# Sixteen-field blocks of a pairwise product: one level of steps replaced by four-by-four products, 18 VectorE instructions a tile instead of 22

## The chip, the cores and the metric

One core of a Trainium2 chip. The experiments ran in three batches on three chips (e1 to e4, e5 to e8, e9 to e11), each with runs of the kernel before on the same chip. The metric is device time in microseconds of one execution. Most executions of a kernel agree within 0.3%.

## The reference

```python
# x: (4096, 32, 64) float32, W: (64, 64) float32
vid = jnp.einsum('bfd,de->bfe', x, W)
idx_i, idx_j = jnp.triu_indices(32, k=1)          # 496 pairs i < j
return x[:, idx_i, :] * vid[:, idx_j, :]          # (4096, 496, 64): 520 MB
```

Some 34 MB go in and 520 MB come out, with one multiplication for each number that is written, besides the product with W, which TensorE does.

## The kernel before

The batch is cut into 16 tiles. In a tile 128 partitions hold the 64 embedding dimensions of two halves of the batch, and the free dimension is fields by C = 128 batch rows. TensorE puts vid for all 32 fields into PSUM. VectorE multiplies x and vid into an output buffer of SLOT = 124 pairs; there are three such buffers, used in turn, and a tile of 496 pairs fills four of them one after the other. SyncE's queue sends each full buffer out (8.13 MB). The order in which pairs are computed is free, since the host puts them in place, so the kernel picks orders that let one instruction do many pairs. A "row" is a rectangle of pairs: each of several fields with the same run of other fields. A "step" is one column of pairs in each of several equal groups of fields.

```python
def by_field():                       # the first two tiles
    return [("row", j, 0, 1, j) for j in range(1, 32)]

def by_block():                       # the other fourteen
    def within(lo):                   # the pairs inside sixteen fields
        yield "step", lo, 2, 1, 0
        for k in range(2):
            yield "step", lo, 4, 2, k
        for k in range(4):
            yield "step", lo, 8, 4, k     # 2 groups x 4 pairs in one instruction
        yield "row", lo + 8, lo, 8, 8     # 8 x 8 pairs in one instruction
    yield from within(0)
    yield "row", 16, 0, 16, 16
    yield from within(16)
...
    opool = ctx.enter_context(tc.tile_pool(name="out", bufs=3))
...
        if 0 < t < NT - 1:
            loaded.append(load(t + 1, 4, nc.scalar))   # four loads of 512 KB
...
            nc.vector.tensor_tensor(o, left, right, ALU.mult)      # line 159
            at += n
            if t * NP + at == until or at in (base + SLOT, NP):
                nc.sync.dma_start(out=out[t][:, sent:at, :],
                                  in_=ot[:, sent - base : at - base, :])
```

A row is split where a buffer ends, which is why a tile had 22 products. The first two tiles send smaller pieces, so that transfers start early.

## Time and profile before

| | before |
|---|---|
| time, median of 3 (range) | 1296.04 us (1294.44 to 1296.83) |
| VectorE busy | 1087.2 us of 1295.9, 376 instructions |
| VectorE idle ahead of line 159, waiting | 124.3 us output landings, 37.3 us "issue", 7.5 us TensorE |
| bytes moved | 553.80 MB, 427 GB/s over the span |
| landing of a full buffer (its transfer is complete) | 43.4 us after its issue |

The second and the fourth row pull in opposite directions: is it the engine that is busy for 84% or the traffic? An average over the span can't say.

### The profile page before, as it was taken

The numbers are of one execution on the slowest core, as the hardware profiler recorded it, in microseconds if no ns is written. First come the engines' busy times: TensorE is split into PE (matmuls) and PEld (weight loads), VectorE is DVE, ScalarE is ACT, GpSimd is POOL, SyncE is SP. The second block draws the span as 40 slices with busy tenths as digits, with TensorE's granted clock in tenths as the row PEclk, the third lists the DMA queues.
The fourth block names the chain that finished last, engine by engine and source line by source line (L and its number), as shares of the span: only waits on it lengthen the run. The fifth ranks groups of instructions, "written<-read, shape, count | busy, mean of one in ns | idle before, by whom it ended". The sixth has DMA issues, their size and how long they took to land.

```text
span 1295.9 us, 1845 instructions
## 1 busy us (share of the span) xinstructions
PE 229.7 (18%) x512; PEld 48.5 (4%) x512; DVE 1087.2 (84%) x376; POOL 0.2 (0%) x4
## 2 busy tenths in 40 slices
PE   4112022112122121221212212122121221212000
PEld 1000000000000000000000000000000000000000
DVE  7999999788798887978879888798897978978870
POOL 0000000000000000000000000000000000000000
PEclk8555555555555555555655555555555555655555
DMA  9999999999999999999999999999999999999996
GB/s 390 431 422 439 427 431 450 432 423 439 430 434 429 425 438 434 424 432 429 435 432 432 433 433 433 434 432 433 435 432 432 431 432 432 430 431 445 437 425 276
DMA packets 20890, 553.80 MB, mean 427 GB/s; under 512 B 2448, under 2 KB 2448, under 8 KB 10256
## 3 DMA queue, kind: packets, MB, share of 16 engines
q1 hardware_dynamic: 12816, 524.33, 93.8%
q10 hardware_dynamic: 8064, 29.36, 5.5%
q8 instruction: 4, 0.07, 0.0%
q14 instruction: 6, 0.05, 0.0%
HBM read 33.59 MB, written 520.09 MB: 427 GB/s over the span
## 4 chain that ended last, share of the span: by engine, by line
DMA 55%; DVE 39%; issue 2%; PE 0%; DVEq 0%; SPq 0%
DMA out_dram<-o 55%; DVE o L159 39%; DMA x<-in_r_x_dram 0%; PE vid L134 0%; DVEq L200 0%; DVEq L159 0%; SPq L111 0%
## 5 line engine op out<-in xcount | busy, mean ns | idle before, releaser
L159 DVE TENSOR_TENSOR o<-x,vid 128x1024 f32<-128x1024 f32 (+15 forms) x376 | 1087.2, 2963 | 169.1 <-DMA out_dram<-o 124.3
L134 PE MATMUL vid<-x,w 64*64 64x512 f32 x512 | 229.7, 1032 | 958.6 <-DMA x<-in_r_x_dram 601.8
L134 PEld LDWEIGHTS vid<-x,w 64*64 64x64 f32 x512 | 48.5, 205 | 1138.1 <-DVE o L159 637.3
L182 POOL MEMSET const-uint8-127<- 128x1 uint8 x1 | 0.1, 103 | 0.0
L182 POOL MEMSET const-bfloat16-1.0<- 128x1 bf16 x1 | 0.1, 102 | 0.0
L182 POOL MEMSET const-float32-1.0<- 128x1 f32 x1 | 0.1, 100 | 0.0
L182 POOL MEMSET const-float32-0.0<- 128x1 f32 x1 | 0.1, 99 | 0.2 <-issue 0.2
## 6 DMA issues: line engine op xcount, KB each, us to landing
out_dram<-o SPq DMA_DIRECT2D x56, 7936.0 KB, 43.4
x<-in_r_x_dram ACTq DMA_DIRECT2D x56, 512.0 KB, 45.5
out_dram<-o SPq DMA_DIRECT2D x2, 3008.0 KB, 18.2
out_dram<-o SPq DMA_DIRECT2D x1, 5952.0 KB, 27.5
out_dram<-o SPq DMA_DIRECT2D x1, 4928.0 KB, 23.6
out_dram<-o SPq DMA_DIRECT2D x1, 4416.0 KB, 19.5
out_dram<-o SPq DMA_DIRECT2D x1, 4224.0 KB, 21.6
out_dram<-o SPq DMA_DIRECT2D x1, 3904.0 KB, 15.8
```

What stands on the lines that cost most here:

```text
L134: nc.tensor.matmul(vid[half, b : b + BANK, :], lhsT=w2[half, :], rhs=xt[half, b : b + BANK, :], start=True, stop=True,)
L159: nc.vector.tensor_tensor(o, left, right, ALU.mult)
L182: nc = _bacc.Bacc("TRN2", target_bir_lowering=False, num_devices=1, dynamic_dma_scratch_size=1024)
```

## The change

The intent is to do the same multiplications in fewer, larger VectorE instructions. Within eight fields, the pairs of the upper four with the lower four are a 4 x 4 block. Before, four "step" instructions did one column of that block each, for both groups of eight fields at once. Now each block is one "row" instruction.

```diff
-        for k in range(4):
-            yield "step", lo, 8, 4, k
+        for i in (lo, lo + 8):
+            yield "row", i + 4, i, 4, 4
```

## The prediction

> **What bounds the kernel now.** I read the page first: busy shares, then the 40 slices, then the chain of waits. After it come the groups of instructions kept apart by shape, the chain in order of time, and ten-microsecond windows over the handover to the blocked tiles and over the end. These are the page's lines:
>
> ```profile
> PE 229.7 (18%) x512; PEld 48.5 (4%) x512; DVE 1087.2 (84%) x376; POOL 0.2 (0%) x4
> ...
> DVE  7999999788798887978879888798897978978870
> ...
> DMA  9999999999999999999999999999999999999996
> GB/s 390 431 422 439 427 431 450 432 423 439 430 434 429 425 438 434 424 432 429 435 432 432 433 433 433 434 432 433 435 432 432 431 432 432 430 431 445 437 425 276
> DMA packets 20890, 553.80 MB, mean 427 GB/s; under 512 B 2448, under 2 KB 2448, under 8 KB 10256
> ...
> DMA out_dram<-o 55%; DVE o L159 39%; DMA x<-in_r_x_dram 0%; PE vid L134 0%; DVEq L200 0%; DVEq L159 0%; SPq L111 0%
> ```
>
> VectorE's 84% tempts one to cut its work. But its row in the slices has gaps from the eighth slice to the end, while the DMA row is 9 in every slice but the last, and moves 422 to 450 GB/s in all but the first and the last. Two engines can't both be the bound; the one without gaps is. The chain says 39% VectorE and 55% output transfer, which needs its order in time (start, length, what):
>
> ```profile
> 899.56 16.76 DVE o L159 x2
> ...
> 1017.58 43.47 DMA out_dram<-o
> 1061.08 0.05 DVEq L159
> 1061.17 16.76 DVE o L159 x2
> 1077.95 43.69 DMA out_dram<-o
> ```
>
> A transfer of 43 us frees a buffer, VectorE fills it in 17 us, its transfer takes 43 us again. A buffer holds 124 products: 124 x 128 x 128 x 4 bytes = 8.13 MB, and at 432 GB/s that is 18.8 us. A landing of 43 us is therefore a queue: the transfer stands behind two others of the three buffers. So the chain's VectorE share is largely not time that VectorE costs: while it fills one buffer, the transfers of the other two are under way or queued.
>
> The period confirms it. The piece at 1061.17 has its like at 899.56, eight buffers or two tiles earlier: (1061.17 - 899.56) / 2 = 80.8 us a tile. A tile moves 496 x 65,536 bytes = 32.51 MB out and 32 x 65,536 = 2.10 MB in, 34.60 MB; over 80.8 us that is 428 GB/s. VectorE has less to do in it. These rows give shape, count, busy us with mean ns, and idle us before it:
>
> ```profile
> L159 DVE TENSOR_TENSOR o<-x,vid 128x14336 f32<-128x14336 f32 x28 | 422.3, 15084 | 44.5 <-DMA out_dram<-o 44.5
> L159 DVE TENSOR_TENSOR o<-x,vid 128x8192 f32<-128x8192 f32 x28 | 243.1, 8681 | 0.0
> L159 DVE TENSOR_TENSOR o<-x,vid 128x1024 f32<-128x1024 f32 x198 | 226.6, 1215 | 38.4 <-issue 37.3 <-DMA out_dram<-o 1.1
> L159 DVE TENSOR_TENSOR o<-x,vid 128x1536 f32<-128x1536 f32 x32 | 56.0, 1750 | 36.7 <-DMA out_dram<-o 36.7
> L159 DVE TENSOR_TENSOR o<-x,vid 128x512 f32<-128x512 f32 x32 | 21.9, 684 | 42.2 <-DMA out_dram<-o 42.0 <-PE vid L134 0.2
> L159 DVE TENSOR_TENSOR o<-x,vid 128x2176 f32<-128x2176 f32 x4 | 9.7, 2415 | 0.0
> L159 DVE TENSOR_TENSOR o<-x,vid 128x1920 f32<-128x1920 f32 x2 | 4.3, 2147 | 0.0
> ```
>
> A blocked tile is 2 x 15.084 + 2 x 8.681 + 14 x 1.215 + 2 x 1.750 + 2 x 0.684 = 69.4 us by these means (67.9 us from first start to last end in the timeline, since neighbours overlap a little). So VectorE idles some 11 to 13 us of each 80.8 us. All of that idle sits ahead of shapes that open a new buffer (14336, 1024, 1536, 512), and none ahead of the 8192 shape, which never does. The part named "issue", 37.3 us in 12 pieces, lies at the first product of a tile, which waits for a buffer, TensorE and VectorE together; with 3.1 us a piece it is as long as the other buffer waits (124.3 us in 40 pieces), and I read it as the same wait.
>
> **What the Trainium skill says.** "Perfetto Trace Analysis", section "Roofline", gives about 435 GB/s as the ceiling of one core's 16 DMA engines when the core beside it is idle. The trace agrees: 429 to 435 GB/s in most slices, and 432 over the 960 us from 220 to 1180. "DMA: Bandwidth & Descriptors", section "Issuing engines are not separate DMA queues", says that transfers issued by different engines interleave on the same 16. The trace fits: loads from ScalarE's queue take 45.5 us for 512 KB, as long as outputs fifteen times larger, and total GB/s stays at the same level. "VectorE: DVE Perf Modes", section "The TRN2 errata", puts an fp32 tensor_tensor of N elements at (N+151)/0.96 ns: 1224 ns for 1024 against 1215 here, so the fixed part of 151/0.96 = 157 ns is nearly confirmed although one operand here is in PSUM.
>
> **The change, part by part.** It touches only the part inside blocks of sixteen fields. Four products of 2 x 4 pairs (1024 elements a partition) become two of 4 x 4 pairs (2048 elements), twice a tile. On TensorE, on ScalarE's and on SyncE's queue the order of instructions and their waits are the same in both programs; on VectorE eight 1024 instructions a tile become four of 2048. The first two tiles, which go field by field, don't change. The bytes, transfers, buffers and cut points of the output don't either: each buffer still ends at 124 products.
>
> Fixed cost of an instruction, from the trace: (15084 - 8681) / 6144 = 1.042 ns an element, and 1215 - 1024 x 1.042 = 148 ns. The new shape is then 2048 x 1.042 + 148 = 2282 ns; the mean of the 1920 and 2176 rows, (2147 + 2415) / 2 = 2281 ns, says the same. Two old ones cost 2430 ns, so each pair saves 148 ns. Fourteen tiles x 4 = 56 instructions fewer: 56 x 0.148 = 8.3 us of VectorE, 0.59 us a tile. Access patterns with one more level cost nothing extra in the trace: 8192 and 14336, which have both operands broadcast over a level, lie on the line of the plain shapes.
>
> Where these 0.59 us lie: 0.3 us in the first buffer of a tile and 0.3 us in the last. Both are between two waits for a landing. From about 212 us to the end VectorE is already ahead, so the wait gets longer by what the work gets shorter: on the path, 0. Before that, from about 130 us, VectorE runs without a gap for one blocked tile. These windows give length, busy times by engine, clock, DMA share, GB/s:
>
> ```profile
> 150.00:160.00 10.00, 0.00 (x0) 0.00 (x0) 10.00 (x3) 0.00 (x0) 0.50 1.00 430
> 160.00:170.00 10.00, 3.68 (x8) 0.84 (x8) 10.00 (x4) 0.00 (x0) 0.50 0.99 420
> 170.00:180.00 10.00, 3.68 (x8) 0.84 (x8) 10.00 (x2) 0.00 (x0) 0.67 1.09 471
> ```
>
> VectorE is full, but so are the transfers, so the 0.59 us of this tile only makes the queue longer: 0 again. At the end, VectorE starts the last buffer at 1239.1 us and finishes at 1256.3. At 1239.1, by the chain in order of time, the transfer of the tile's first buffer has landed and two remain: 2 x 18.8 us, so the last one could start at about 1276.7, 20 us after it was issued, and end at about 1295.5, which is the span. Being issued 0.3 us earlier doesn't end it earlier. Sum on the path: 0 to -0.6 us.
>
> **The rivals.** First, VectorE bounds after all, as 84% busy and 39% of the chain suggest, and the whole 8.3 us shows: 1287.7 us, 0.64% less. Against it: 161.6 us of waits for buffers, in 52 of the 56 buffers of the blocked tiles. Even so it would be within 2%. Second, the 4 x 4 form runs slower than the line, through broadcasts on both operands: at twice the rate cost, 56 x 2.13 = 119 us more VectorE work, 8.5 us a tile, still under the idle of 11 to 13 us, so about 1298 us. The 8 x 8 shape, built by the same branch of the code, speaks against it. Third, the shift in reads frees PSUM and x earlier or later and loads collide differently with outputs. VectorE waited on TensorE only twice, 7.5 us in total, at the start, and fields 4 to 7 and 20 to 23 are released sooner, so TensorE can only gain slack; bytes are the same, and I give this 1 us either way. Fourth, the slowest of the DMA engines decides the end: the last windows fall from 444 to 165 GB/s at 1280 us, with single packets to the end, so engines don't finish together. That tail may vary by some microseconds from run to run, and is the largest part of my range.
>
> ```profile
> 1270.00:1280.00 10.00, 0.00 (x0) 0.00 (x0) 0.00 (x0) 0.00 (x0) 0.50 1.02 444
> 1280.00:1290.00 10.00, 0.00 (x0) 0.00 (x0) 0.00 (x0) 0.00 (x0) 0.50 0.38 165
> ```
>
> **Range and chances.** The centre is 1296.0 less half of 0.6, rounded: 1295.7 us. The three runs before spread over 2.4 us, another chip or day may add as much, and the first rival would take up to 8 us off: 1292 to 1299 us. Over 2% faster would need 26 us, three times all that the change removes from VectorE, so 0.005; over 2% slower needs the new form to cost well beyond the second rival, about 0.01. Within 2%: 0.985.
>
> **What would show it.** VectorE x320 and not x376; busy 1087.2 - 8.3 = 1078.9 us, a share of 83%; 56 of the new 2048 shape near 2282 ns and 86 of 1024; VectorE's idle up from 169.1 to about 177 us, nearly all on output landings; the tile period still 80.8 us; the DMA row still 9; output landings still near 43 us, and the wait ahead of the last buffer longer by about 0.3 us. I am wrong if the period falls by about 0.6 us a tile (first rival), if the 2048 rows are near 4000 ns (second), or if GB/s in the middle slices moves from about 432 (third).

## The result, and the profile after

The changed kernel took 1294.8 us (median of 4, 1292.93 to 1296.52) beside 1295.24 us (1293.92 to 1296.83) of the kernel before. The ratio is 0.9996, with an interval of 0.9977 to 1.0015: the same.

The page of the changed kernel, with the parts that answer to those shown before: busy time, slices, traffic, chain.

```profile
PE 227.8 (18%) x512; PEld 48.5 (4%) x512; DVE 1083.6 (84%) x320; POOL 0.2 (0%) x4
...
DVE  7999999888898887888879788798887988979870
...
DMA  9999999999999999999999999999999999999996
GB/s 393 429 423 438 429 432 435 430 431 434 433 434 431 432 433 435 433 435 436 433 431 436 431 433 431 435 434 431 431 431 434 431 433 427 427 431 438 438 430 302
...
DMA out_dram<-o 55%; DVE o L159 39%; DMA x<-in_r_x_dram 0%; PE vid L134 0%; DVEq L200 0%; DVEq L159 0%; SPq L111 0%
```

The 56 instructions are gone, and nothing else looks different: the same gaps in VectorE's row, a full DMA row, the same rate, the same shares of the chain. But busy time fell by 3.6 us only (1087.2 to 1083.6), not by 8.3. The groups kept apart by shape (count, then busy us with mean ns, then idle ahead) show that the new shape cost what was expected of it:

```profile
L159 DVE TENSOR_TENSOR o<-x,vid 128x2048 f32<-128x2048 f32 x56 | 125.4, 2280 | 0.0
L159 DVE TENSOR_TENSOR o<-x,vid 128x1024 f32<-128x1024 f32 x86 | 99.8, 1215 | 40.3 <-issue 38.1 <-DMA out_dram<-o 2.2
```

The mean of 2280 ns is within 2 ns of the prediction. Busy time is not count times mean here, though: 56 x 2.280 = 127.7, and the row says 125.4; for 1024 elements 86 x 1.215 = 104.5, and the row says 99.8. The first number counts the time that instructions cover together, and neighbours overlap. The timeline of VectorE shows it for the last buffer of the run, start and length first, then the count and the wait ahead. This is the kernel before:

```profile
1239.11 17.20 DVE L159 TENSOR_TENSOR o<-x,vid 128x512 f32<-128x512 f32 x9 [1.92 <-DMA out_dram<-o]
```

And this the changed one:

```profile
1236.53 17.07 DVE L159 TENSOR_TENSOR o<-x,vid 128x512 f32<-128x512 f32 x7 [1.93 <-DMA out_dram<-o]
```

Two instructions fewer shorten the same 124 products by 0.13 us, 65 ns each. The earlier start can't be put down to the change from one pair of profiles: it is the 2.5 us by which the two profiled executions differ as a whole, and executions of the kernel before alone lay between 1292.54 and 1296.64 us in one batch. The chain in order of time has its old rhythm:

```profile
897.72 16.76 DVE o L159 x2
...
1015.74 43.26 DMA out_dram<-o
...
1059.12 16.76 DVE o L159 x2
1075.90 43.57 DMA out_dram<-o
```

Two tiles take 1059.12 - 897.72 = 161.40 us, 80.7 us a tile, where the kernel before took 80.8. A saving on the path of 0.26 us a tile (3.6 us over 14) is the size of the differences between neighbouring periods, so this view alone can't exclude it. The experiments have to.

### The profile page after: what moved, and what is told of

The parts are those of the page before. It is cut to its first block, busy times and chain, and to the rows that moved or that the text cites. A ratio compares the mean times of both kernels' runs of the same rounds, so it can differ in the third digit from the quotient of the medians.

```text
span 1293.4 us, 1789 instructions
## 1 busy us (share of the span) xinstructions
PE 227.8 (18%) x512; PEld 48.5 (4%) x512; DVE 1083.6 (84%) x320; POOL 0.2 (0%) x4
## 4 chain that ended last, share of the span: by engine, by line
DMA 55%; DVE 39%; issue 2%; PE 0%; DVEq 0%; SPq 0%
DMA out_dram<-o 55%; DVE o L159 39%; DMA x<-in_r_x_dram 0%; PE vid L134 0%; DVEq L200 0%; DVEq L159 0%; SPq L111 0%
## 5 line engine op out<-in xcount | busy, mean ns | idle before, releaser
L159 DVE TENSOR_TENSOR o<-x,vid 128x2048 f32<-128x2048 f32 (+13 forms) x320 | 1083.6, 3454 | 170.0 <-DMA out_dram<-o 124.2
```

## The experiments

Labels e1 to e11 are the order of the runs; here they are grouped by question. Theory: the 16 DMA engines bound the kernel from some 5 us after the start to the end; VectorE has about 3 us to spare in each of the 56 buffers, so neither adding nor removing less than that changes the time. Rival 1: VectorE bounds, wholly or in part, and the saving was just too small to see. A second question is why the saving was 3.6 us and not 8.3: the theory formed from the trace is that the mean duration of an instruction holds some 83 ns that lie over its neighbour, so that an instruction removed gives back only about 65 ns.

### More and less work for VectorE

Extra products go to a spare tile, K of them in each buffer of the fourteen blocked tiles. VectorE's own order was fixed to that of the program, which leaves the changed kernel's instructions as they were.

```diff
             nc.vector.tensor_tensor(o, left, right, ALU.mult)
+            if t >= 2 and at == base:
+                for _ in range(K):
+                    nc.vector.tensor_tensor(extra, xt[:, 0:8, :], xt[:, 8:16, :], ALU.mult)
```

K = 2 (e1):

> The changed kernel with two extra VectorE products of 1024 elements in each of the 56 buffers of the blocked tiles, written to a spare tile. The result stays correct. Each extra product waits for the one before, so a pair costs about 2.4 us a buffer, 56 x 2.4 = 134 us of VectorE. Theory (the 16 DMA engines bound, VectorE idles 2.9 us a buffer): all of it goes into the idle, which falls from 170 to about 35 us; time 1295 us, within 4 us of the kernel before. Rival (VectorE bounds): 1294.8 + 134, about 1429 us.

Measured: 1297.21 us (1294.62 to 1297.47), ratio to the kernel before 1.0011 (0.9995 to 1.0028), so the same. VectorE's busy time rose from 1083.6 to 1214.7 us. Here are the page's busy line and VectorE's waits for this run (line 159 has become 160; us in total, times, longest):

```profile
PE 224.7 (17%) x512; PEld 51.4 (4%) x512; DVE 1214.7 (94%) x432; POOL 0.2 (0%) x4
```

```profile
DVE o L160 <- DMA out_dram<-o: 26.9, 28, 2.8
DVE o L160 <- PE vid L135: 8.4, 2, 7.8
DVE o L160 <- issue: 6.9, 10, 0.8
```

The waits of the changed kernel were 124.2, 7.7 and 38.1. So 131 us of added work came out of 128 us of waiting, and the time hardly moved. It also fits the reading of "issue" as a wait for buffers: it shrank together with the named one, from 3.2 us a piece to 0.7.

K = 5 (e2):

> As the run with two extra products, but five in each buffer: about 6.1 us a buffer, 343 us of VectorE, more than the idle of 162 us that lies ahead of buffers. Theory: VectorE becomes the bound, its waits for landings go to about 0 and the time is 1295 + (343 - 162) + some us, 1450 to 1490 us. Rival (VectorE bounded all along): 1295 + 343, about 1638 us.

Measured: 1455.48 us, ratio 1.1238. VectorE's work rose by 333 us against the changed kernel; the time by 161 us. Now the two rows of the slices change roles:

```profile
DVE  7999999999999999999999999999999999999994
...
DMA  9999998979889888898987988979899797897878
```

The gaps are in the DMA row, and this trace has no wait for an output landing at all. With some 7.6 us of short gaps, the last product ended at 1432.4 us and not at 1253.6, 178.8 us later: the work added (333.4) less the waits that it filled (162.2), and the gaps. About 19 us came back at the end, where fewer transfers were still queued after that product (21 us from there to the end of the span, and 39.8 in the changed kernel). Together the two runs place the threshold between 131 and 333 us of added work, with the position that the idle time gives, 162 us, explaining the second to within its tail.

The other direction takes work away from VectorE, far more than the change did: the two large products of each tile become ScalarE copies (e4).

```diff
-            nc.vector.tensor_tensor(o, left, right, ALU.mult)
+            if t >= 2 and m == 7:
+                nc.scalar.copy(o, left)          # wrong result on purpose
+            else:
+                nc.vector.tensor_tensor(o, left, right, ALU.mult)
```

> The changed kernel with the two 14336-element products of each blocked tile taken from VectorE; ScalarE, which was idle, copies x into their place (wrong result on purpose). VectorE loses 28 x 15.08 = 422 us, a third of the span; bytes and buffers stay. Theory: the time stays within 5 us of 1295 us and VectorE's idle grows by about 420 us. Rival (VectorE's share of the chain is real cost): a fall by up to 39% of the span, at least by 100 us.

Measured: 1296.2 us (1292.47 to 1296.85), ratio 0.9998 (0.9976 to 1.0021). VectorE was busy for 663.9 us, 51% of the span, and waited 583.2 us for output landings:

```profile
PE 228.8 (18%) x512; PEld 48.4 (4%) x512; DVE 663.9 (51%) x292; ACT 341.2 (26%) x29; POOL 0.2 (0%) x4
```

```profile
DVE o L162 <- DMA out_dram<-o: 583.2, 54, 18.6
```

A hundred times the saving of the change also bought nothing, within the 3 us that the interval leaves open. That is the strongest reading of what VectorE's work costs. It has a limit: a copy took ScalarE 12.1 us, so in 28 of the 56 buffers the filling became shorter by 4.6 us only (16.75 to 12.1) and did not vanish.

### The change undone and more (e5)

```diff
-        for ... in products(by_field() if t < 2 else by_block()):
+        for ... in products(by_field()):
```

> The change undone and more: all sixteen tiles go field by field, 34 products a tile and not 18, with the same bytes and buffers. 14 x 16 = 224 instructions more. At the marginal 65 ns that the two traces give (3.6 us of busy time for 56 instructions) it is 14.6 us of VectorE, at the 148 ns of the prediction 33 us; the idle of 162 us takes either. Theory: same as before, 1294 to 1297 us, VectorE busy about 1098 us (at 148 ns: 1117 us). Rival (VectorE bounds): 1309 to 1328 us.

Measured: 1297.33 us (1294.84 to 1299.1) beside 1296.1, ratio 1.0016 (0.9999 to 1.0033): the same, and a tenth of a per cent can't be excluded: the median is 0.3 us above the range expected. This is not the kernel before: the whole blocked order is gone, and not the change alone. VectorE's busy time was 1097.9 us, 14.3 us over the changed kernel: 14.3 / 224 = 64 ns an instruction, and not the 148 ns of the prediction.

### Fewer bytes (e3)

```diff
-            loaded.append(load(t + 1, 4, nc.scalar))
+            loaded.append(loaded[t - 1])        # wrong result on purpose
```

> The changed kernel without the 14 loads of x after the first two tiles; the later tiles use the x of the first two, so the result is wrong on purpose and the VectorE instructions are the same. Bytes fall by 14 x 2.10 = 29.4 MB. Theory: time falls by 29.4 MB at 432 GB/s, 68 us, to about 1227 us, and VectorE's idle falls by about as much. Rival (VectorE bounds): no change, 1295 us.

Measured: 1219.6 us in both runs, ratio 0.9417. With VectorE's work unchanged (1083.2 us) the time fell by 75 us, and so did VectorE's idle (170.0 to 94.8). The bytes explain 68 us; the direction settles what bounds the kernel, the size was missed by 7 us. The slices show where these are:

```profile
GB/s 385 428 435 427 431 433 434 434 434 434 434 436 434 432 434 434 434 434 434 434 432 434 432 432 434 434 434 434 434 434 432 432 434 430 434 434 432 434 430 390
```

The last slice moves 390 GB/s, and 302 in the changed kernel. Against 432 GB/s these are 3.0 and 9.7 us lost, so the end explains the 7 us. Without loads, the DMA engines finish close together; with loads, the rate falls off over the last 15 us or so (127 and then 13 GB/s in the last two windows of 5 us), which I read as engines that straggle. Two runs tried to find out why.

Loads on the outputs' queue (e9):

```diff
-            loaded.append(load(t + 1, 4, nc.scalar))
+            loaded.append(load(t + 1, 4, nc.sync))
```

> The changed kernel with the loads of x issued on SyncE's queue, where the outputs are, and not on ScalarE's. Same bytes and packets. In the profile of both kernels the DMA engines end unevenly (the last 15 us move 133 to 254 GB/s and less), while the run without loads ended evenly and fell by 75 us where its bytes explain 68. If the mix of two queues lets some of the 16 engines fall behind: the end gets even and the time falls by 5 to 8 us, to 1287 to 1291 us, and a slice at the end like that of the run without loads. If the small packets of the loads are the reason, or nothing is: 1294 to 1297 us.

Loads in one transfer (e10):

```diff
-            loaded.append(load(t + 1, 4, nc.scalar))
+            loaded.append(load(t + 1, 1, nc.scalar))
```

> The changed kernel with each later load of x in one transfer of 2 MB and not four of 512 KB, so packets of 16 KB and not 4 KB, still on ScalarE's queue. A 4 KB packet took 160 ns, 25.6 GB/s an engine, a 63 KB packet 2347 ns, 27.05 GB/s. If packet size is the reason for the 7 us: 1289 to 1292 us. If the mix of queues is: no change in the uneven end, 1293 to 1297 us.

Both missed. On the outputs' queue: 1300.5 us, ratio 1.0045 (1.0028 to 1.0061), with 250 GB/s in the last slice. In one transfer: 1306.64 us, ratio 1.0086 (1.0068 to 1.0104), with 253. Their intervals lie above 1: slower, with an end that is less even. So neither the mix of two queues nor the small packets alone make the engines straggle, and four loads on ScalarE's queue were the better choice. The last slice accounts for only about 4 us of either loss. The rest lies earlier: in e9 before 220 us (421 GB/s, and 427 in the changed kernel), most of it at 85 to 95 us (318 and 329 GB/s, and 404 and 456), just after the first four loads took 5.04 us to issue on SyncE's queue with outputs behind them; in e10 through the middle too (430 GB/s from 220 to 1000 us, and 433).

The run with two output buffers (e11, below) says more than these two. It has the loads as in the changed kernel, and ends evenly:

```profile
GB/s 389 429 427 436 439 422 413 415 425 411 421 442 406 433 411 420 442 415 423 413 421 442 404 435 411 421 442 411 429 412 420 441 416 439 429 413 431 421 434 403
```

The uneven end went away when the loads were left out, and also when a third buffer was. In these profiles it needs both; how it comes about, and which engines are late, stays open: these traces don't tell the 16 engines apart.

### The saving where it counts

To see in the time what an instruction costs, VectorE must be the bound. Sending only half of each full buffer does that, for three orders of products.

```diff
+                end = at if t < 2 else sent + SLOT // 2     # wrong result on purpose
                 nc.sync.dma_start(
-                    out=out[t][:, sent:at, :],
-                    in_=ot[:, sent - base : at - base, :],
+                    out=out[t][:, sent:end, :],
+                    in_=ot[:, sent - base : end - base, :],
```

The new form, the old form, and field by field:

> The changed form (18 products) in a kernel that sends only the first half of each full buffer in the blocked tiles (wrong result on purpose: half of the output isn't written). A tile then moves 16.3 + 2.1 MB, 42.5 us at 432 GB/s, less than VectorE's 67.6 us, so VectorE should be the bound: about 1100 us, no waits for landings. Taken with the run of the old form in the same kernel: the theory of 65 ns an instruction says the old form is 3.6 us longer (0.33%), the prediction's 148 ns says 8.3 us (0.75%); if VectorE's time never mattered, no difference.

> The old form (22 products) in the kernel that sends half of each full buffer. Against the new form in the same kernel: 3.6 us longer by the marginal cost of 65 ns, 8.3 us longer by the 148 ns of the prediction.

> Field by field (34 products) in the kernel that sends half of each full buffer. 224 instructions more than with 18: 14.6 us longer (1.3%) by the marginal 65 ns, 33 us longer (3%) by the prediction's 148 ns.

Measured, on one chip (e6, e7, e8): 1100.61 us (1100.36 to 1100.64) with 18 products, 1103.99 us (1103.9 to 1104.12) with 22, and 1106.9 us (1106.61 to 1107.06) with 34. The runs of each form now agree within 0.5 us, and the old form is 3.38 us longer: 3.38 / 56 = 60 ns an instruction. VectorE's timeline is one piece from start to end. With 18 and with 22:

```profile
9.28 1077.89 DVE L159 TENSOR_TENSOR o<-x,vid 128x512 f32<-128x512 f32 x317 [0.58 <-PE vid L134]
```

```profile
8.96 1081.51 DVE L159 TENSOR_TENSOR o<-x,vid 128x512 f32<-128x512 f32 x373 [0.41 <-PE vid L134]
```

The piece is 3.62 us longer, 65 ns for each of 56; it also started 0.32 us earlier, which takes that much off the difference in time. The change does what it was made for; there is just nothing to gain from it in the kernel as it is.

The third form was expected 14.6 us over the first, and is 6.3 us over it. Its piece on VectorE has the expected length:

```profile
9.06 1092.36 DVE L159 TENSOR_TENSOR o<-x,vid 128x512 f32<-128x512 f32 x541 [0.62 <-PE vid L134]
```

1092.36 - 1077.89 = 14.5 us, 65 ns an instruction. But VectorE ends at 1101.4 us of a span of 1104.8, where the first form ends at 1087.2 of 1098.8: 3.4 us to the end and not 11.6. This comes from the experiment. The half that is sent holds the first 62 products of the last buffer; in the order by field these are done two products before the end, so the last transfer is already running while VectorE finishes, and in the blocked order the 8 x 8 product that fills the buffer's end also reaches into its first half. The expectation had left out the tail: 14.5 - 8.2 = 6.3.

### One buffer fewer (e11)

```diff
-    opool = ctx.enter_context(tc.tile_pool(name="out", bufs=3))
+    opool = ctx.enter_context(tc.tile_pool(name="out", bufs=2))
```

> The changed kernel with two output buffers and not three. Theory: the chain's VectorE share costs nothing because other transfers are queued behind; with two buffers, one transfer (18.8 us, and 1.2 us for its share of the loads) still covers the fill of 17.0 us but with about 1 us to spare for a landing and an issue[...]. So up to 1 to 2 us for each of 56 buffers may show: 1300 to 1400 us, and output landings of 22 to 25 us and not 43. If VectorE's and the transfer's parts of the chain added up: 37 us a buffer, above 2000 us.

Measured: 1312.15 us (1311.39 to 1313.49), ratio 1.0133 (1.0114 to 1.0152): the interval lies above 1, so it is slower. Landings took 22.6 us. This is the row of the changed kernel, and then this run's (KB each, median us to landing):

```profile
out_dram<-o SPq DMA_DIRECT2D x56, 7936.0 KB, 43.1
```

```profile
out_dram<-o SPq DMA_DIRECT2D x56, 7936.0 KB, 22.6
```

Fill and transfer of a buffer don't add up to the time, as the two alternating in the chain might suggest; one other transfer in flight covers nearly all of the fill. A buffer's share of the period is 80.8 / 4 = 20.2 us, so the 43 us in the chain were the transfer itself, the one before it in full, and the last 3 us of the one before that.

## Why the prediction was right

**What bounds the kernel: right, and shown.** The time followed the bytes (e3) and not VectorE's work, which was varied from 664 to 1215 us without effect (e4, e1) and set the time only beyond the idle that the profile shows (e2). Whether the 16 engines or the memory behind them set the rate, no run here tells apart.

**The chain's 39% isn't VectorE's cost: right.** Removing 420 us of that work left the time where it was (e4), and with two buffers the landing halved for 1.3% of time (e11). The prediction's "stands behind two others" counts one that was nearly done: three transfers of 20.2 us would make 61 us, and the landing took 43.

**The saving of 8.3 us: wrong, 3.6 us.** The term that failed is "each pair saves 148 ns". The fit through the mean durations was sound: the 2048 row came out at 2280 ns. The error was to add up mean durations as if instructions followed each other end to end. Four measurements agree on what one instruction less is worth: 64 ns of busy time in the changed kernel (3.6 / 56), 64 ns by field (14.3 / 224), 65 ns from the piece on VectorE's timeline, and 60 ns of time where VectorE bounds. The prediction had the hint in hand: it gave a tile as 69.4 us by means and 67.9 us by the clock, said that neighbours overlap, and then used the means. The 1.5 us between them, over the 18 joints inside the four buffers, are 83 ns a joint, and 148 - 83 = 65. The Trainium skill has this in "Perfetto Trace Analysis", section "Optimizing Scalar/DVE Operations": about 60 ns for VectorE on SBUF as engine time, with a profiled latency about twice that, because the write acknowledgement overlaps the next instruction. The trace agrees with both figures, 65 and 148 ns; that the overlap is the write acknowledgement, no run here shows.

**On the path 0 to -0.6 us: right as far as it can be measured, the sum for the end with luck.** The result's interval, -0.23% to +0.15%, is 3 us down and 2 us up, so it alone would not tell 0.6 from 2 us; e1 and e4 do, by steps 36 and 116 times as large, if the effect goes with the size. The sum for the end (from 1239.1 us, three transfers of 18.8 us make 1295.5) meets the span, but not in the way it says. From 1239.1 us on, the profile moves 343 GB/s over 56.8 us, 19.5 MB and not the 24.4 MB of three buffers: 4.9 MB had gone ahead, and the uneven end (169 GB/s from 1276.7 us) took that time back.

**VectorE's idle "up to about 177 us": wrong with its term.** It is 170.0 us, from 169.1. With 3.6 us less work in a span 2.5 us shorter, 170.2 was due. The wait ahead of the last buffer is 1.93 us after 1.92, not 0.3 us longer.

**The rivals.** The first fell with e1 and e4. The second, a slow 4 x 4 form, fell with the 2280 ns. The third, other collisions of loads and outputs, left no sign in the rate of the middle slices. The fourth, DMA engines that end unevenly, is real and unexplained: it was worth about 7 us in e3, more than the whole change. Whether it makes the spread from run to run, for which the range was kept, was not tested.

## What to carry to other kernels

Before cutting an engine's work, find which row of the slices has no gaps, and add up the waits of the engine in question ahead of its buffers. Here these were 162 us in 52 waits; 131 us of added work cost nothing that could be measured, and 420 us removed gained nothing. To price an instruction, take the difference in busy time or in the length of a gapless stretch between two variants, not the mean duration of a row, which here held 148 ns of fixed cost where 60 to 65 ns could be saved. And to see whether a change works at all, run it once in a version of the kernel in which its engine is the bound.

## What the Trainium skill lacked or had wrong

- "VectorE: DVE Perf Modes", section "The TRN2 errata": (N+151)/0.96, given there for an fp32 add, is near the duration of one instruction as the profile reports it here for a product (1224 ns by the page, 1215 here for N = 1024). It isn't what an instruction adds in a row of them: 60 to 65 ns beside the time for its elements. The page's table has a row near that, 58 + FD/Accel cycles (58/0.96 = 60 ns, by the page), but says of it only that it falls short of the duration of a single instruction, not that it is what one more instruction in a row adds.
- "Perfetto Trace Analysis", section "Optimizing Scalar/DVE Operations", has about 125 ns for VectorE on PSUM, and doesn't say which figure holds for mixed operands. With one operand in PSUM, the other and the output in SBUF, the cost was that of its SBUF figure, 60 to 65 ns.
- "DMA: Bandwidth & Descriptors", section "Issuing engines are not separate DMA queues": by the page, issuing from several engines saves only issue time, which is usually small. The runs don't contradict that, but show that it can count: moving the loads from ScalarE's to SyncE's queue made this kernel slower by 0.45% (0.28 to 0.61%). Some 3 us of it lie before 220 us, where four loads took 5.04 us to issue ahead of outputs; the rest stays open.
- No page that I read says that a queue of three 8 MB stores beside small loads ends unevenly, over some 15 us (302 GB/s in the last slice, and 390 without the loads or 403 with two buffers), nor that merging the loads into 2 MB transfers makes it worse (253 GB/s in the last slice; the kernel was 0.86% slower, mostly before the end).
